# First attention of a hybrid block on one core: a chunk's scores in nine full steps, the diagonal blocks in two steps of their own, the later half of the queries first

## The chip, the core and the metric

The kernel runs on one core of a Trainium2 chip. The number that counts is the device time of one execution in microseconds (us). The five engines of a core that appear below are PE (TensorE, the matrix unit; PEld is its weight load), DVE (VectorE), ACT (ScalarE), POOL (GpSimd) and SP (SyncE, which here only issues DMAs). Each engine works through its own list of instructions in order. A matrix product writes into PSUM, eight banks of 512 fp32 columns on 128 partitions; DVE and ACT read it from there.

## What is computed

A block with four parts, each added to its input: attention A, an expert feed-forward part, attention B, and the same feed-forward part again. Only attention A is touched. It has 1024 tokens, 32 heads of 16 channels, rotary embedding and a causal mask:

```python
xq = rotary_pos_emb((x @ wq.T).reshape(B, T, n_heads, hd))
xk = rotary_pos_emb((x @ wk.T).reshape(B, T, n_heads, hd))
xv = (x @ wv.T).reshape(B, T, n_heads, hd)
scores = jnp.einsum('bqhd,bkhd->bhqk', xq, xk) * hd ** (-0.5)
scores = jnp.where(causal[None, None], scores, NEG_INF)
probs = jax.nn.softmax(scores, axis=-1)
out = jnp.einsum('bhqk,bkhd->bqhd', probs, xv).reshape(B, T, C) @ wo.T
```

## The kernel before

**Chunks.** The 32 heads are worked in eight chunks of four (`NCA` is 8, `HC` is 4). In `qT` and `kT` a chunk fills the 128 partitions with four strips of 32: 16 channels of a head, one row for the maximum, and zeros. A score product of one head therefore uses 32 rows of the matrix unit, and four heads in different strips run beside each other.

**Scores twice.** Softmax needs each query's maximum. The kernel makes every score twice. The *row* scores (`row_scores`, L310) have queries on partitions; DVE takes the maxima from them (`maxima`, L327 for a block without the mask, L330 for one with it). `with_maxima` (L345 to L350) turns the negated maxima of one half of the queries into rows (a transpose on PE, `tp_m`; a copy on ACT; four DMAs from SP) and writes them into the spare row of `qT`, where `kT` has ones. The *column* scores (`col_scores`, L362) have keys on partitions and get the maximum subtracted by that row. `exponentials` adds the causal mask with a bf16 product against the identity (L380) and lets ACT take the exponential into `p` (L382). `product` (L396) multiplies `p` with the values and a column of ones into `oT`, one PSUM bank (`ps_o`, one buffer) for the 512 queries of a half. When a half is done ACT copies it (L407), and `normalize` transposes it on PE (`tp_o`, L99), divides by the sums on DVE and POOL.

**Steps.** Queries come in halves `qc` of 512, keys and queries in blocks of 128. The lists `by_rows` and `by_cols` say what a step makes: a pair `(i, kc)` is row block `i` against the key half `kc`, a pair `(qc, b)` is key block `b` against query half `qc`, as wide as the mask leaves it (512, 384, 256 or 128). There are ten steps; two of them, n = 2 and n = 9, are 256 wide on both sides, the others 512. The order is the earlier half of the queries first (n = 0 to 2), then the later half (n = 3 to 9). The mask goes to the first 128 columns of each block on the diagonal: one such block in n = 0, 2, 7 and 9, two in n = 1 and 8.

**Half-steps.** While chunk c makes its column scores, chunk c+1 makes its row scores in the same step. `step` does so in two half-steps: column scores of heads 2 and 3 with row scores of heads 0 and 1, then the other way round. On PE a half-step is: the four score products beside each other, the mask products of two heads (if the step is on the diagonal), what is due (`tp_o`, `tp_m`), and half of the product of the step before the last. The score tiles come from a pool of seven banks, so that the four tiles of a half-step wait for banks of the two half-steps before it, which ACT or DVE has to have read.

**Ends.** The row scores of chunk 0 have no partner; they stand between the projections (three steps with the last query and key projections, seven with value projections `pj_v`). The last chunk makes column scores of all four heads at once, with no half-steps. `with_maxima` for the earlier half is done in step 5 of the rows, for the later half in step 1 of the next chunk; the column scores need them in step 0 and step 3.

Of the kernel before, what the change touches and what calls it, by code (L numbers as in the profile page):

```python
# [9 lines left out]
F32 = mybir.dt.float32  # L10
# [6 lines left out]
P = 128  # L17
# [47 lines left out]
class Block:  # L65
# [174 lines left out]
    def attend_a(self, ctx_pool, pt, work, ps_s, ps_o, qT, kT, v_p, project_qk, project_v, midway, tail):  # L240
        nc, tc = self.nc, self.tc
        HC = P // PADA
        with ExitStack() as ctx:
# [22 lines left out]

            by_rows = [[(3, 0)], [(2, 0), (0, 0)], [(1, 0)], [(4, 0)], [(5, 0)], [(6, 0)], [(7, 0)]]
            by_rows += [[(7, 1)], [(6, 1), (4, 1)], [(5, 1)]]  # L270
            by_cols = [[(0, 0)], [(0, 1), (0, 3)], [(0, 2)], [(1, 0)], [(1, 1)], [(1, 2)], [(1, 3)]]
            by_cols += [[(1, 4)], [(1, 5), (1, 7)], [(1, 6)]]
            NP = len(by_rows)
            negs, parts, outs = {}, {}, {}

            def neg(c, half):
# [15 lines left out]
                    yield *x, at, at + width(*x)  # L292
                    at += width(*x)

            def row_pieces(n):
                return list(placed(by_rows[n], lambda i, kc: min(QC, (i + 1) * P - kc * QC)))

            def col_pieces(n):
                return list(placed(by_cols[n], lambda qc, b: min(QC, (qc + 1) * QC - b * P)))

            def on_diagonal(qc, b):
                return b * P >= qc * QC

            def row_scores(c, n, heads, made):

                for j in heads:
                    made[j] = ps_s.tile([P, QC], F32, tag="s", name=f"s{c}_{n}_{j}")
                for i, kc, at, end in row_pieces(n):
                    for j in heads:
                        nc.tensor.matmul(  # L310
                            made[j][:, at:end],
                            lhsT=qT[rows_of(j), c, i * P : (i + 1) * P],
                            rhs=kT[rows_of(j), c, kc * QC : kc * QC + end - at],
                            start=True,
                            stop=True,
                        )
                        yield

            def maxima(c, n, heads, made):

                for j in heads:
                    for i, kc, at, end in row_pieces(n):
                        s, w = made[j][:, at:end], end - at
                        if i >= NT // 2 and kc == 0:
                            if (c, i) not in parts:
                                parts[c, i] = qk.tile([P, HC], F32, tag="part", name=f"part{c}_{i}", bufs=8)
                            nc.vector.tensor_reduce(parts[c, i][:, j : j + 1], s, AX.X, ALU.max, negate=True)  # L327
                            continue
                        junk = work.tile([P, QC], F32, tag="w", name=f"junk{c}_{i}_{j}")
                        nc.vector.tensor_tensor_reduce(  # L330
                            out=junk[:, :w],
                            in0=s,
                            in1=mask[:, QC - w :],
                            scale=-1.0,
                            scalar=parts[c, i][:, j : j + 1] if kc else -NEG,
                            op0=ALU.add,
                            op1=ALU.min,
                            accum_out=neg(c, i // 4)[:, j, i % 4 : i % 4 + 1],
                        )
# [14 lines left out]

            def col_scores(c, n, heads, made):

                pieces = col_pieces(n)
                for j in heads:
                    made[j] = ps_s.tile([P, QC], F32, tag="s", name=f"sT{c}_{n}_{j}")
                for x, (qc, b, at, end) in enumerate(pieces):  # L360
                    for j in heads:
                        nc.tensor.matmul(  # L362
                            made[j][:, at:end],
                            lhsT=kT[rows_of(j), c, b * P : (b + 1) * P],
                            rhs=qT[rows_of(j), c, (qc + 1) * QC - (end - at) : (qc + 1) * QC],
                            start=x == 0,
                            stop=x == len(pieces) - 1 and not on_diagonal(qc, b),
                        )
                        yield

            def exponentials(n, heads, made, p):
                pieces = col_pieces(n)
                end = pieces[-1][-1]

                if on_diagonal(*pieces[0][:2]):
                    step = pieces[-1][2] // P or 1
                    mask = maskT.unsqueeze(1).to_broadcast([P, len(pieces), P])
                    for j in heads:
                        to = made[j].rearrange("p (a k) -> p a k", k=P)[:, : (len(pieces) - 1) * step + 1 : step, :]
                        nc.tensor.matmul(to, lhsT=identb, rhs=mask, start=False, stop=True)  # L380
                for j in heads:
                    nc.scalar.activation(p[:, j, :end], made[j][:, :end], AF.Exp)  # L382

            def product(c, n, p):

                first, last = n in (0, 3), n in (2, NP - 1)
                pieces = col_pieces(n)
                qc, middle = pieces[0][0], pieces[-1][-1] // 2
                if first:
                    outs[c, qc] = ps_o.tile([P, QC], F32, tag="o", name=f"oT{c}_{qc}")  # L390
                o = outs[c, qc]
                for lo, hi in ((0, middle), (middle, 2 * middle)):
                    for _, b, at, end in pieces:
                        x0, x1 = max(lo, at), min(hi, end)
                        for j in range(HC if x0 < x1 else 0):
                            nc.tensor.matmul(  # L396
                                o[rows_of(j), QC - end + x0 : QC - end + x1],
                                lhsT=v_cols(b, c * HC + j),
                                rhs=p[:, j, x0:x1],
                                start=first and x0 == 0,  # L400
                                stop=last and x1 == 2 * middle,
                            )
                    yield
                if not last:
                    return
                oT = work.tile([P, QC], F32, tag="w", name=f"oTs{c}_{qc}")
                nc.scalar.copy(oT, o)  # L407
                later.append(lambda: normalize(c, qc, oT))

            def normalize(c, qc, oT):  # L410
                if not o_sb:
# [25 lines left out]
            later = []  # L437
            pending = []

            def step(rc, cc, n):  # L440


                p, made, madeT = None, {}, {}
                due = list(later)
                later.clear()
                if cc is not None:
                    p = pt.tile([P, HC, QC], F32, tag="p", name=f"p{cc}_{n}")
                    pending.append((cc, n, p))
# [2 lines left out]
                for half in range(2 if both else 1):  # L451
                    rows, cols = (2 * half, 2 * half + 1), (2 - 2 * half, 3 - 2 * half)
                    if not both:
                        rows = cols = range(HC)
                    gens = []
                    if cc is not None:
                        gens.append(col_scores(cc, n, cols, madeT))
                    if rc is not None:
                        gens.append(row_scores(rc, n, rows, made))
                    drain(gens)  # L460
                    if rc is not None:
                        maxima(rc, n, rows, made)
                    if cc is not None:
                        exponentials(n, cols, madeT, p)
                    while due:
                        due.pop(0)()
                    next(turns, None)
                drain([turns])
                if rc is not None and n == 4:
                    later.append(lambda: with_maxima(rc, 0))  # L470
                if cc is not None and n == 0:
                    later.append(lambda: with_maxima(cc, 1))


            for i in range(1, NT):
# [4 lines left out]
                next(project_v)  # L480
                step(0, None, n)
            for _ in project_v:
                pass
            for c in range(NCA):
                if c == NCA // 2:
                    midway()
                for n in range(NP):
                    step(c + 1 if c + 1 < NCA else None, c, n)
            for item in pending:
                drain([product(*item)])  # L490
            tail(o_sb, ps_s, work, later)
        return o_sb
# [493 lines left out]
def hybrid_block_kernel(  # L986
# [38 lines left out]
    def tail(o, ps, work, later):  # L1025
        oTs = [gather(o, i, work, ps, "w", "s") for i in range(2)]
        out_projection(0, oTs[0], ps, "s")
        while later:
            later.pop(0)()
        out_projection(1, oTs[1], ps, "s")  # L1030

    weights = [w_baseT, w_rhT, lora_B, b_base]
# [105 lines left out]
```

## Time and profile before

| | us |
|---|---|
| median of 3 runs (lowest, highest) | 1655.16 (1654.3, 1655.9) |
| the profiled execution | 1654.29 |
| its span, first to last instruction | 1652.2 |
| PE, DVE, ACT, POOL busy in the span | 1632.8, 1100.7, 555.2, 351.6 |
| chunk 0's first column scores | 119.12 |
| chunks 0 to 7 begin at | 119.12, 154.10, 190.71, 227.32, 263.94, 300.55, 337.16, 373.76 |
| the transposes that follow attention A (`tp_ao`) begin at | 401.31 |

The granted clock of TensorE is 1.000 for the whole span. A chunk's begin is the first column score product of its step 0 in the timeline. In the timeline a row begins with its start and its length in us; a row with x2 or more is several instructions run together. Each fp32 product of scores stands there as two passes. The length of a PE row holds its way through the array, so that the distance of two starts, not the length, tells what a product costs. Lines of code are those printed above.

### The profile page before, as it was taken

Reading aid. Unit: us, or ns where it says so; the run is one execution under the profiler, and the core shown is the slowest. Engines: PE = TensorE matmul, PEld = TensorE weight load, DVE = VectorE, ACT = ScalarE, POOL = GpSimd, SP = SyncE. Lnnn points to the kernel's source line nnn. Section 1 sums busy time; section 2 is a strip of 40 time slices with the busy share of each in tenths; the row PEclk is TensorE's granted clock in tenths of the full one; section 3 lists DMA queues with packets and bytes.
Section 4 is the critical chain, followed back from the end, with each engine's and each line's share of the span. In section 5 each row is a group of like instructions: output and inputs, shape, how many; then the busy total and the mean of one; then the engine's idle time right before and its main releaser. Section 6 shows DMA issues by size and latency. Waiting matters only on the chain.

```text
span 1652.2 us, 31905 instructions
## 1 busy us (share of the span) xinstructions
PE 1632.8 (99%) x12920; PEld 937.4 (57%) x12920; DVE 1100.7 (67%) x2832; ACT 555.2 (34%) x1230; POOL 351.6 (21%) x524
## 2 busy tenths in 40 slices
PE   9999999999999999999999999999999999999998
PEld 5544444444654657556655765655665576556654
DVE  4557777771553886776677677677667767777762
ACT  2325565555212333233233223223323322332230
POOL 3000000001311332223213222222322222222140
PEclk9999999999999999999999999999999999999999
DMA  5000000001003200200200120020020012000001
GB/s 198 1 1 2 3 2 2 2 2 40 1 27 88 65 1 27 65 27 26 65 27 7 51 60 2 27 65 26 27 65 26 16 45 64 1 27 27 2 1 51
DMA packets 60866, 52.03 MB, mean 31 GB/s; under 512 B 5744, under 2 KB 47472, under 8 KB 60720
## 3 DMA queue, kind: packets, MB, share of 16 engines
q1 hardware_dynamic: 59408, 46.06, 9.7%
q0 software_dynamic: 784, 2.90, 0.5%
q8 instruction: 101, 1.65, 0.4%
q10 hardware_dynamic: 528, 1.05, 0.2%
q14 instruction: 45, 0.37, 0.1%
HBM read 30.98 MB, written 2.10 MB: 20 GB/s over the span
## 4 chain that ended last, share of the span: by engine, by line
PE 95%; DVE 3%; ACT 1%; POOL 1%; issue 0%; ACTq 0%; DVEq 0%; POOLq 0%
PE s L798 15%; PE pq L752 13%; PE o L842 13%; PE wo L649 12%; PE sT L362 8%; PE kv L707 7%; PE oT L396 5%; PE pm_f L606 3%; PE or L842 3%; PE s L310 2%; PE pj_v L185 2%; PE pj_q L185 2%; PE pj_k L185 2%; PE sT L380 1%; PE pm_ao L1022 1%; PE st L778 1%
## 5 line engine op out<-in xcount | busy, mean ns | idle before, releaser
L807 ACT ACTIVATE p<-p,nm 128x1024 f32<-128x1024 f32 (+7 forms) x256 | 198.2, 774 | 405.3 <-DVE nm L805 363.6
L810 POOL TENSOR_SCALAR p<-p,rs 128x1024 f32<-128x1024 f32 (+7 forms) x256 | 190.9, 747 | 644.8 <-DVE rs L809 620.9
L798 PE MATMUL s<-kT,qT 128*128 128x512 f32 (+3 forms) x768 | 296.0, 493 | 1.9 <-DVE p L800 1.8
L825 DVE STREAM_TRANSPOSE pT<-p 128x640 f32<-128x640 f32 (+4 forms) x256 | 169.0, 670 | 128.6 <-PE o L842 84.5
L752 PE MATMUL pq<-xnTb,wq 128*128 128x512 f32 x512 | 243.0, 597 | 0.0
L649 PE MATMUL wo<-wo,oT 128*128 128x512 f32 x512 | 240.7, 593 | 1.8 <-DVE nm L805 1.8
L800 DVE SCALAR_TENSOR_TENSOR p<-s,rq,rel 128x512 f32<-128x512 f32 (+3 forms) x384 | 223.9, 601 | 24.6 <-PE s L798 23.4
L798 PEld LDWEIGHTS s<-kT,qT 128*128 128x128 f32 x768 | 140.8, 190 | 164.8 <-issue 117.7
L842 PEld LDWEIGHTS o<-pT,va 32*128 32x128 f32 x5248 | 210.7, 185 | 25.5 <-issue 17.9
L842 PE MATMUL o<-pT,va 32*128 32x256 f32 (+5 forms) x5248 | 220.0, 321 | 0.0
L382 ACT ACTIVATE p<-sT 128x512 f32<-128x512 f32 (+1 forms) x320 | 159.2, 554 | 107.1 <-PE sT L380 67.6
L804 DVE TENSOR_REDUCE nm<-p 128x1 f32<-128x1024 f32 (+7 forms) x256 | 188.7, 738 | 2.9
L310 PE MATMUL s<-kT,qT 32*128 32x512 f32 (+3 forms) x768 | 169.6, 524 | 0.0
L362 PE MATMUL sT<-qT,kT 32*128 32x512 f32 (+3 forms) x768 | 160.5, 524 | 0.0
L649 PEld LDWEIGHTS wo<-wo,oT 128*128 128x128 f32 x512 | 94.6, 190 | 89.0 <-issue 76.3
L752 PEld LDWEIGHTS pq<-xnTb,wq 128*128 128x128 f32 x512 | 92.4, 190 | 88.8 <-issue 79.7
L707 PE MATMUL kv<-wkv,xnTb 128*128 128x256 f32 x512 | 116.5, 380 | 0.8 <-DVE qT L762 0.5
L707 PEld LDWEIGHTS kv<-wkv,xnTb 128*128 128x128 f32 x512 | 96.3, 190 | 20.0 <-issue 4.0
L327 DVE TENSOR_REDUCE part<-s 128x1 f32<-128x512 f32 x128 | 82.0, 685 | 36.9 <-PE s L310 31.0
L362 PEld LDWEIGHTS sT<-qT,kT 32*128 32x128 f32 x768 | 61.5, 183 | 56.3 <-issue 37.8
L396 PE MATMUL oT<-p,v_p 128*32 128x256 f32 (+1 forms) x1408 | 93.0, 350 | 0.0
L421 POOL TENSOR_TENSOR o<-os,rsa 128x64 f32<-128x64 f32 x64 | 16.7, 293 | 338.5 <-DVE rsa L419 323.4
(154 smaller groups left out, 1623.2 us busy)
## 6 DMA issues: line engine op xcount, KB each, us to landing
va<-v SPq DMA_DIRECT2D x256, 64.0 KB
wq<-in_b_WqT_dram SPq DMA_DIRECT2D x8, 1024.0 KB
wo<-in_b_WoT_dram SPq DMA_DIRECT2D x8, 1024.0 KB
x<-in_x_dram SPq DMA_DIRECT2D x8, 256.0 KB
wkv<-in_b_WkT_dram SPq DMA_DIRECT2D x8, 256.0 KB
wkv<-in_b_WvT_dram SPq DMA_DIRECT2D x8, 256.0 KB
out_dram<-x SPq DMA_DIRECT2D x8, 256.0 KB
wq<-in_a_wqT_dram ACTq DMA_DIRECT2D x1, 1024.0 KB
```

The source lines that it names most:

```text
L310: nc.tensor.matmul(made[j][:, at:end], lhsT=qT[rows_of(j), c, i * P : (i + 1) * P], rhs=kT[rows_of(j), c, kc * QC : kc * QC + end - at], s ...
L362: nc.tensor.matmul(made[j][:, at:end], lhsT=kT[rows_of(j), c, b * P : (b + 1) * P], rhs=qT[rows_of(j), c, (qc + 1) * QC - (end - at) : (qc ...
L396: nc.tensor.matmul(o[rows_of(j), QC - end + x0 : QC - end + x1], lhsT=v_cols(b, c * HC + j), rhs=p[:, j, x0:x1], start=first and x0 == 0, ...
L649: nc.tensor.matmul(ps, lhsT=oTs[g, h][:, t * P : (t + 1) * P], rhs=wo[:, h, :], start=(h == heads[0]), stop=(h == heads[-1]))
L707: nc.tensor.matmul(ps.rearrange("p a b -> p (a b)"), lhsT=xnT[:, kc, i * P : (i + 1) * P], rhs=wkv[:, kc].rearrange("p a b -> p (a b)"), s ...
L752: nc.tensor.matmul(ps, lhsT=wq[:, kc, hh * DB : (hh + 1) * DB], rhs=xnT[:, kc, cols], start=(kc == 0), stop=(kc == KC - 1))
L798: nc.tensor.matmul(s, lhsT=qT[:, i * P : (i + 1) * P], rhs=kT[:, lo:hi], start=True, stop=True)
L800: nc.vector.scalar_tensor_tensor(p[:, lo:hi], s, rq[:, i : i + 1], rel[:, at + lo : at + hi], ALU.mult, ALU.add)
L804: nc.vector.tensor_reduce(nm, p[:, :w], AX.X, ALU.max, negate=True)
L807: nc.scalar.activation(p[:, :w], p[:, :w], AF.Exp, bias=nm, scale=slope, accum_out=ss)
L810: nc.gpsimd.tensor_scalar(p[:, :w], p[:, :w], rs, 1.0, ALU.mult, ALU.mult)
L842: nc.tensor.matmul(cols(o[:, a], j), lhsT=vs[g][rows, j * NB + b, :], rhs=moving(j, rows, slice(b * B, (b + 1) * B)), start=(j == js[0] an ...
```

## The change

`by_rows` and `by_cols` become functions of the chunk. There are nine steps where rows and columns go together. The four diagonal blocks of a query half (128 x 128 each) make one step of their own, `diagonal(qc)`; what stands beside them, to the right of the diagonal, makes `beside(qc, ...)`: blocks 0 and 2 (384 + 128) in one step, block 1 (256) in another. Every chunk but the last takes `down_cols`: the later half of the queries first, and the two 256-wide remainders, `beside(1, 1)` and `beside(0, 1)`, in one step. The last chunk takes `up_cols`: ten steps, the earlier half first. Rows of chunks 0 and 7 follow `up_rows`, the others `down_rows`; in both, (1, 0) and (5, 1) share a step. The mask is added once a diagonal step, over 512 columns for a head. `product` finds out itself where a half begins and ends; in the merged step its first half ends `qc` = 1 and its second half opens `qc` = 0. `with_maxima` is queued after the last step that a half's rows need, and is done in the first half-step after that; the queue `later` is now looked through in every half-step.

```diff
-            by_rows = [[(3, 0)], [(2, 0), (0, 0)], [(1, 0)], [(4, 0)], [(5, 0)], [(6, 0)], [(7, 0)]]
-            by_rows += [[(7, 1)], [(6, 1), (4, 1)], [(5, 1)]]
-            by_cols = [[(0, 0)], [(0, 1), (0, 3)], [(0, 2)], [(1, 0)], [(1, 1)], [(1, 2)], [(1, 3)]]
-            by_cols += [[(1, 4)], [(1, 5), (1, 7)], [(1, 6)]]
+            up_rows = [[(3, 0)], [(2, 0), (0, 0)], [(4, 0)], [(5, 0)], [(1, 0), (5, 1)], [(6, 0)], [(7, 0)], [(7, 1)]]
+            up_rows += [[(6, 1), (4, 1)]]
+            down_rows = [[(4, 0)], [(5, 0)], [(6, 0)], [(7, 0)], [(7, 1)], [(6, 1), (4, 1)], [(1, 0), (5, 1)], [(3, 0)]]
+            down_rows += [[(2, 0), (0, 0)]]
+            def diagonal(qc):
+                return [(qc, 4 * qc + a, a * P, (a + 1) * P) for a in range(4)]
+            def beside(qc, *blocks):
+                return [(qc, 4 * qc + a, (a + 1) * P, QC) for a in blocks]
+            full = [[(1, b, 0, QC)] for b in range(4)]
+            up_cols = [diagonal(0), beside(0, 0, 2), beside(0, 1), *full, diagonal(1), beside(1, 0, 2), beside(1, 1)]
+            down_cols = [*full, diagonal(1), beside(1, 0, 2), beside(1, 1) + beside(0, 1), diagonal(0), beside(0, 0, 2)]
+            def by_rows(c):
+                return up_rows if c in (0, NCA - 1) else down_rows
+            def by_cols(c):
+                return down_cols if c < NCA - 1 else up_cols
...
-                if on_diagonal(*pieces[0][:2]):
-                    step = pieces[-1][2] // P or 1
+                if pieces[0][:4] in diagonal(pieces[0][0]):
                     mask = maskT.unsqueeze(1).to_broadcast([P, len(pieces), P])
                     for j in heads:
-                        to = made[j].rearrange("p (a k) -> p a k", k=P)[:, : (len(pieces) - 1) * step + 1 : step, :]
+                        to = made[j].rearrange("p (a k) -> p a k", k=P)
                         nc.tensor.matmul(to, lhsT=identb, rhs=mask, start=False, stop=True)
...
                 for lo, hi in ((0, middle), (middle, 2 * middle)):
+                    for qc, b, x0, _, at, end in pieces:
+                        p0, p1 = max(lo, at), min(hi, end)
+                        if p0 >= p1:
+                            continue
+                        first = (c, qc) not in outs
+                        if first:
+                            outs[c, qc] = ps_o.tile([P, QC], F32, tag="o", name=f"oT{c}_{qc}")
...
+                        if last:
+                            oT = work.tile([P, QC], F32, tag="w", name=f"oTs{c}_{qc}")
+                            nc.scalar.copy(oT, o)
+                            later.append([0, lambda qc=qc, oT=oT: normalize(c, qc, oT)])
                     yield
...
+            def due():
+                for x in list(later):
+                    x[0] -= 1
+                    if x[0] < 0:
+                        later.remove(x)
+                        x[1]()
...
-                if rc is not None and n == 4:
-                    later.append(lambda: with_maxima(rc, 0))
-                if cc is not None and n == 0:
-                    later.append(lambda: with_maxima(cc, 1))
+                if rc is not None:
+                    for half in range(2):
+                        if n == max(m for m, y in enumerate(by_rows(rc)) for x in y if x[0] // 4 == half):
+                            later.append([0, lambda half=half: with_maxima(rc, half)])
...
             for _ in project_v:
-                pass
+                due()
             for c in range(NCA):
                 if c == NCA // 2:
                     midway()
-                for n in range(NP):
+                for n in range(len(by_cols(c))):
                     step(c + 1 if c + 1 < NCA else None, c, n)
             for item in pending:
+                due()
                 drain([product(*item)])
```

## The prediction

> **What bounds the kernel now.** I first read the windows, one for each chunk (bounds are the starts of the first column score product of a chunk; columns: length, then the busy time of PE, PEld, DVE, ACT, POOL).
>
> ```profile
> core 0: us, PE busy (x) PEld busy (x) DVE busy (x) ACT busy (x) POOL busy (x), PEclk, DMA share, GB/s
> ...
> 154.10:190.71 36.61, 36.33 (x406) 15.76 (x402) 25.89 (x83) 21.78 (x47) 2.09 (x8) 1.00 0.01 2
> 190.71:227.32 36.61, 36.34 (x406) 15.77 (x402) 25.88 (x83) 21.77 (x47) 2.09 (x8) 1.00 0.01 3
> ```
>
> Chunks 1 to 6 take 36.61 us each, to 0.02. PE is busy 99% of it, DVE 71%, ACT 59%, at full clock, and the page's chain of waits is 95% PE. So a chunk costs what PE's list costs, plus small waits that the busy time hides. To see both I read the timeline of one plain pair of half-steps (n = 3):
>
> ```profile
> 202.20 0.69 PE L362 MATMUL sT<-qT,kT 32*128 32x512 f32 x1
> ...
> 203.27 0.64 PE L396 MATMUL oT<-p,v_p 128*32 128x256 f32 x8
> ...
> 203.42 1.08 ACT L382 ACTIVATE p<-sT 128x512 f32<-128x512 f32 x2 [1.08 <-PE s L310]
> 203.84 0.69 PE L362 MATMUL sT<-qT,kT 32*128 32x512 f32 x1
> ...
> 204.07 0.69 PE L310 MATMUL s<-kT,qT 32*128 32x512 f32 x1
> ...
> 205.12 0.65 PE L396 MATMUL oT<-p,v_p 128*32 128x128 f32 x16
> ...
> 205.69 0.69 PE L362 MATMUL sT<-qT,kT 32*128 32x512 f32 x1
> ```
>
> Four score products of 512 columns side by side: 203.27 - 202.20 = **1.07** (call it S). Half of a value product: 203.84 - 203.27 = **0.57** (P), and 205.69 - 205.12 = 0.57 too where it is sixteen passes of 128 columns instead of eight of 256. The fourth score tile of the second half-step starts at 204.07 and not 203.84: its bank is read by the first exponential, 203.42 to 203.96. So S is 1.28 there, a wait of **0.2**. That pushes the next half-step back far enough not to wait itself; two plain half-steps take 205.69 - 202.20 = 3.49, and n = 6 takes 1.79 + 1.70 = 3.49 too. Then the masks (n = 7 and 8):
>
> ```profile
> 217.60 0.28 PE L380 MATMUL sT<-maskT,identb 128*128 128x128 bf16 x2
> 217.81 0.64 PE L396 MATMUL oT<-p,v_p 128*32 128x256 f32 x8
> ...
> 221.04 0.27 PE L362 MATMUL sT<-qT,kT 32*128 32x128 f32 x1
> ...
> 221.15 0.27 PE L362 MATMUL sT<-qT,kT 32*128 32x128 f32 x1
> ...
> 221.46 0.39 PE L380 MATMUL sT<-maskT,identb 128*128 128x256 bf16 x2
> 221.78 0.64 PE L396 MATMUL oT<-p,v_p 128*32 128x256 f32 x8
> ```
>
> The masks of two heads (M) cost 0.21 at 128 columns and 0.32 at 256, all of it on PE's path. A 128-wide score piece follows the one before on its strip after 0.11.
>
> From the same timeline: S of a 256-wide step 0.65, P of one 0.36, `tp_o` alone (T) 0.58, `tp_m` (X) 0.22. A chunk's account: S 16 x 1.07 + 4 x 0.65 = 19.72; P 16 x 0.57 + 4 x 0.36 = 10.56; M 8 x 0.21 + 4 x 0.32 = 2.96; T 1.16; X 0.44; together 34.84, so 1.77 of waits.
>
> **The change, part by part, for a chunk with both sides.**
>
> *Nine full steps for ten.* S becomes 18 x 1.07 = 19.26 (-0.46), P 18 x 0.57 = 10.26 (-0.30). The value products on 128-wide pieces cost no more, by the 0.57 above.
>
> *Masks.* Twelve half-steps with a mask become four, each with 512 columns a head. The trace has no such mask. The rows give 0.11 for 128 more columns on both heads, so 0.32 + 2 x 0.11 = 0.54. Below, it is no shorter than the 256-wide 0.32; above, no longer than four 128-wide pairs, 4 x 0.21 = 0.84. I take 0.54, on the line of both rows: M = 4 x 0.54 = 2.16 (-0.80). The bounds move a chunk by -0.9 to +1.2.
>
> *Diagonal steps.* A head has four pieces of 128 where it had one of 512, eight passes of 0.11, 0.88 in all, on a strip of its own, beside row products of 512 that need 1.07 anyhow. They are hidden, S stays 1.07: no gain is possible under the row products. If a 128-wide piece could not load its weights under the piece before, every pass would cost two times 0.11 and S about 1.07 + 8 x 0.11 = 1.9. The 0.11 between two such pieces in the fence above, each with weights of its own, says they can.
>
> *Waits.* DVE's heaviest half-step, (6, 1) with (4, 1), takes 1.70 in its timeline (221.47 to 223.17); (1, 0) with (5, 1) is put together from 256-wide rows, 2 x (0.35 + 0.41) = 1.52. Both are under the 1.74 of a plain half-step, so DVE doesn't become late although they now stand next to each other without masks between. The built program's list of waits shows that the last score tile of most half-steps still waits for the first exponential of the half-step before, so I keep 0.2 in every second plain half-step: seven of nine steps, 1.4. In diagonal half-steps the exponential starts later, but PE too: 0.54 of mask and 0.57 of product stand before the next scores, against about 0.5 + 0.54 until the first exponential is done: no wait. After X, 0.2 for DVE's second maximum. With 0.1 after T that is 1.7, as before.
>
> *T and X* are as many as before. X for the later half moves from the next chunk's n = 1 to n = 7, one half-step after the maxima it needs. These end 1.22 + 1.52 = 2.74 after their half-step's begin; PE gets to X, a plain half-step, S and M later, after 1.64 + 1.07 + 0.54 = 3.25: no wait. In the queue it then stands in front of one P and the second diagonal half-step; they would be late with it. Before, X at 232.44 was followed by the ACT copy at 233.56 and SP's first of four DMAs, spaced 0.67, and all had landed 4.7 after X. Now 0.57 + 2.19 + 3.5 + 0.6 = 6.9 us lie between X and the chunk's first column scores, so SP's four DMAs, each behind the other in SP's queue, stay hidden with 2 us to spare. The earlier half has six steps.
>
> *The merged step.* Its second P opens a new `oT` in the one bank. ACT has to have copied the old one: its exponentials end 2.30 after that step's begin in PE's next round (n = 8), the copy takes 0.59, T stands at 1.64 + 1.07 + 0.2 = 2.91. It is ready just then; if not, ACT's 0.1 to 0.3 is paid once a chunk.
>
> *Sum for a chunk:* 19.26 + 10.26 + 2.16 + 1.16 + 0.44 + 1.7 = 35.0, that is **-1.6**. Chunks 1 to 6: -9.6. Chunk 0 has no value products in its first two steps, before and after, and one X less: -1.8.
>
> *The ends.* Chunk 0 now needs the later half's maxima at once. X comes after the seventh value projection; the copy, the DMAs and their landing take 0.9 + 0.25 + 3.3 = 4.45, the X and the last projection, 0.2 + 3.6, cover 3.8: +0.65, once (0 to 1.5). The rows before it lose one half-empty step: -0.1. In the last chunk M is paid in two lumps of 4 x 0.28, in which ACT, at 2.07 of exponentials a step, has nothing to do, and X comes a step earlier, which takes away most of the wait at 382.3 to 383.6 for its DMAs; I put it at 0 (-1.5 to +1).
>
> Together -9.6 - 1.8 + 0.65 - 0.1 = **-10.8**. The profiled execution took 1654.29 us (span 1652.2): 1643.5. Taken from the median of the runs, 0.87 higher: **1644.4**. Everything behind attention A starts earlier by the same time; it is 99% PE and waits for nothing that has another clock, since its weights are loaded in buffers that attention A frees.
>
> **The rivals.**
>
> 1. *Weights don't hide under short pieces* (slower). A diagonal half-step then costs 0.85 more, 4 x 7 + 2 of them: +25.5, 1669.9. From 0.36 more per half-step on, the change loses. Against it stands the 0.11 between passes, on all four strips at once; for it, that the trace shows only one such piece after another on a strip, not four. The Trainium skill, TensorE: Matmul & The Clock Gate, "The mechanism", states this rule: a weight load overlaps with running products only when they are on other strips. By that rule the gap would be 0.21; the trace's 0.11 doesn't agree.
> 2. *The gain goes into PSUM waits.* If the 0.2 is paid in every plain half-step and not in every second, 7 more a chunk: 1.4 x 7 = 9.8, 1654: no change. If in half of them, 1649. For it: masks gave ACT time in twelve half-steps and now do in four. Against it: the pair always comes to 3.49 in the trace.
> 3. *The maxima come late.* The order is turned round and the column scores of the later half are wanted right at a chunk's begin. If the DMAs land 1 us after that instead of 2 before it, 7 us are lost: 1651. Against it: the 4.7 above, the same in every chunk.
>
> **How the numbers follow.** Forecast 0.72, with its own range 1640 to 1649 (the mask's bounds weighted to its line, the ends' bounds). Rival 1: 0.08. Rival 2: 0.12, half of it no change. Rival 3: 0.05. The remaining 0.03 is a slowdown I don't see. The range 1639 to 1653 leaves out rival 1, a part of rival 2 and what is unseen. A measurement of this kernel can tell about 0.2%, 3.3 us. Faster by more: 0.72 + 0.06 + 0.04 = 0.82. Within: 0.07. Slower: 0.11.
>
> **What would show it.** Chunks 1 to 5 begin 35.0 apart (34.4 to 35.6). The mask rows are 8 instructions a chunk, 0.27 to 0.28 from one to the next. The value product after a diagonal step's masks begins 1.6 to 1.7 after the first column score; 2.4 there means rival 1. Plain pairs at 3.6 or more mean rival 2. A gap of PE ahead of a chunk's first column score, ended by a DMA, means rival 3. The forecast is wrong if chunks are not shorter than 36.

## The result and the profile after

| us | before | changed |
|---|---|---|
| median of 4 runs (lowest, highest) | 1655.15 (1654.3, 1655.9) | 1641.41 (1639.48, 1641.65) |
| the profiled execution, its span | 1654.29, 1652.2 | 1641.65, 1639.6 |
| attention A: first column score to `tp_ao` | 119.12 to 401.31: 282.19 | 119.95 to 387.08: 267.13 |
| of it chunk 0, chunks 1 to 6, last chunk | 34.98, 219.66, 27.55 | 32.15, 208.76, 26.22 |
| from `tp_ao` to the last matmul | 1246.20 | 1247.89 |

The ratio of the times is 0.9915, 95% interval 0.9897 to 0.9932: 13.7 us less by the medians. The forecast was 1644.4.

The windows of the changed kernel by chunk, columns as before (bounds are again the first column score products): chunk 0, chunks 1 and 2, and the last one.

```profile
core 0: us, PE busy (x) PEld busy (x) DVE busy (x) ACT busy (x) POOL busy (x), PEclk, DMA share, GB/s
119.95:152.10 32.15, 32.15 (x390) 18.16 (x390) 24.73 (x79) 20.68 (x40) 0.00 (x0) 1.00 0.01 2
152.10:186.78 34.68, 34.68 (x454) 17.73 (x451) 25.69 (x85) 21.30 (x43) 2.09 (x8) 1.00 0.01 2
186.78:221.46 34.68, 34.68 (x454) 17.74 (x450) 25.68 (x85) 21.29 (x43) 2.09 (x8) 1.00 0.01 3
360.86:387.08 26.22, 24.37 (x429) 13.87 (x426) 1.17 (x7) 20.37 (x46) 3.13 (x12) 1.00 0.01 2
```

A chunk takes 34.68 where it took 36.61; PE is busy in all of it and has more instructions (454 for 406: the 128-wide pieces). DVE and ACT do what they did (25.7 and 21.3 for 25.9 and 21.8). Chunks 3 and 5 take 34.69 and 34.68, chunks 4 and 6 take 34.96 and 35.07. In chunk 4 one exponential starts 0.28 later in its half-step than in chunk 2, and the scores behind it take 1.56 for 1.29; why it is late stays open. Chunk 6 makes the rows of the last chunk, by `up_rows`, so that X stands in another step, and the scores behind it take 1.71.

The timeline of the changed kernel in two plain half-steps, the first with X, then one more begin:

```profile
186.78 0.69 PE L378 MATMUL sT<-qT,kT 32*128 32x512 f32 x1
...
187.85 0.28 PE L360 MATMUL tp_m<-ident,neg 128*16 128x128 f32 x1
188.00 1.09 ACT L397 ACTIVATE p<-sT 128x512 f32<-128x512 f32 x2 [1.11 <-PE s L325]
...
188.06 0.65 PE L417 MATMUL oT<-p,v_p 128*32 128x128 f32 x16
...
188.63 0.69 PE L378 MATMUL sT<-qT,kT 32*128 32x512 f32 x1
...
190.35 0.69 PE L378 MATMUL sT<-qT,kT 32*128 32x512 f32 x1
```

S is 187.85 - 186.78 = 1.07 and P 188.63 - 188.06 = 0.57, as before. The pair takes 190.35 - 186.78 = 3.57 with X's 0.21 in it; without X, plain pairs take 3.43 to 3.51. So X costs about 0.1 of its 0.21 there (0.06 to 0.14, by the pair it is held against). The rest fits time in which the next half-step would have waited for a bank. The diagonal half-step in the same kernel's timeline:

```profile
203.47 0.37 PE L378 MATMUL sT<-qT,kT 32*128 32x128 f32 x1
203.48 0.69 PE L325 MATMUL s<-kT,qT 32*128 32x512 f32 x1
...
203.68 0.51 PE L378 MATMUL sT<-qT,kT 32*128 32x128 f32 x6
...
204.03 0.60 PE L378 MATMUL sT<-qT,kT 32*128 32x128 f32 x7
...
204.57 0.60 PE L395 MATMUL sT<-maskT,identb 128*128 128x512 bf16 x2
...
205.00 1.08 ACT L397 ACTIVATE p<-sT 128x512 f32<-128x512 f32 x2 [1.06 <-PE sT L395]
...
205.10 0.64 PE L417 MATMUL oT<-p,v_p 128*32 128x256 f32 x8
...
205.68 0.58 PE L378 MATMUL sT<-qT,kT 32*128 32x384 f32 x1
```

The 128-wide pieces (x1, x6, x7, and more in lines left out) follow each other inside the time of the row products: S is 204.57 - 203.47 = 1.10. The mask (M) then takes 205.10 - 204.57 = 0.53.

Summed over every half-step of a chunk's timeline (work is a count times 1.07 or 0.65, the wait is what S takes beyond it):

| us per chunk | S work | waits in S | P | M | T waiting for ACT's copy | T + X | sum |
|---|---|---|---|---|---|---|---|
| before | 19.72 | 1.60 | 10.54 | 2.92 | 0.34 | 1.49 | 36.61 |
| changed | 19.26 | 1.52 | 10.28 | 2.05 | 0 | 1.58 | 34.69 |

### The profile page after: what moved, and what is told of

Read it like the earlier page. It is cut to its first block, busy times and chain, and to the rows that moved or that the text cites. A ratio compares the mean times of both kernels' runs of the same rounds, so it can differ in the third digit from the quotient of the medians.

```text
span 1639.6 us, 32629 instructions
## 1 busy us (share of the span) xinstructions
PE 1621.2 (99%) x13320; PEld 955.1 (58%) x13320; DVE 1099.2 (67%) x2832; ACT 551.5 (34%) x1202; POOL 350.8 (21%) x524
## 4 chain that ended last, share of the span: by engine, by line
PE 73%; DVE 3%; POOL 1%; ACT 1%; issue 0%; ACTq 0%; DVEq 0%
PE s L825 15%; PE pq L779 14%; PE o L869 13%; PE wo L676 13%; PE kv L734 7%; PE pm_f L633 3%; PE or L869 3%; PE pm_ao L1049 1%; PE st L805 1%; PE pm_f L634 1%; PE tp_k L99 0%; DVE p L827 0%; PE pr_f L568 0%; PE oT L417 0%; POOL x L559 0%; DVE pT L852 0%
## 5 line engine op out<-in xcount | busy, mean ns | idle before, releaser
L397 ACT ACTIVATE p<-sT 128x512 f32<-128x512 f32 (+1 forms) x292 | 155.7, 592 | 97.7 <-PE s L325 46.2
L325 PE MATMUL s<-kT,qT 32*128 32x512 f32 (+3 forms) x768 | 164.1, 520 | 0.0
L378 PE MATMUL sT<-qT,kT 32*128 32x128 f32 (+3 forms) x1152 | 155.4, 401 | 0.2 <-DMA qT<-negT 0.2
L378 PEld LDWEIGHTS sT<-qT,kT 32*128 32x128 f32 x1152 | 80.9, 184 | 50.8 <-issue 24.6
L417 PE MATMUL oT<-p,v_p 128*32 128x128 f32 (+1 forms) x1552 | 89.8, 332 | 0.0
```

The lines of the kernel that those rows point to most:

```text
L325: nc.tensor.matmul(made[j][:, at:end], lhsT=qT[rows_of(j), c, i * P : (i + 1) * P], rhs=kT[rows_of(j), c, kc * QC : kc * QC + end - at], s ...
L378: nc.tensor.matmul(made[j][:, at:end], lhsT=kT[rows_of(j), c, b * P : (b + 1) * P], rhs=qT[rows_of(j), c, qc * QC + x0 : qc * QC + x1], st ...
```

## The experiments

Every experiment starts from the changed kernel, whose chunk is 34.69 and whose attention A is 267.13 by its profile. Chunks and attention A are read from one profile each; a chunk's time is that of chunks 1 to 3, which agree to 0.02. Total times of single runs are given beside them; these differ by some 1.7 us by whether the execution has the half-clock stretch of the last section, so that attention A is what is compared.

### Is the mask paid by the instruction or by the half-step?

```diff
-                    mask = maskT.unsqueeze(1).to_broadcast([P, len(pieces), P])
-                    for j in heads:
-                        to = made[j].rearrange("p (a k) -> p a k", k=P)
-                        nc.tensor.matmul(to, lhsT=identb, rhs=mask, start=False, stop=True)
+                    for a in range(4):
+                        for j in heads:
+                            to = made[j][:, a * P : (a + 1) * P]
+                            nc.tensor.matmul(to, lhsT=identb, rhs=maskT, start=False, stop=a == 3)
```

> The changed kernel with one edit: in a diagonal step the mask of a head is added in four products of 128 columns instead of one of 512. Nothing else moves. In the changed kernel chunks 1 to 5 begin 34.69 us apart and the masks of a half-step (M) take 0.54. Theory A: a masked half-step pays once for turning the array from strips to whole and back (about 0.10), and then for columns alone (0.056 for 128 columns of a head): M = 0.10 + 8 x 0.056 = 0.55, chunks 34.7 (34.6 to 34.9). Theory B: each mask product has a price of its own, as the pairs of 0.21 before the change read: M = 4 x 0.21 = 0.84, four half-steps, chunks 35.9.

Chunk 34.73, attention A 267.52, total 1639.94. The timeline of this kernel's diagonal half-step, mask and then value product:

```profile
202.05 0.62 PE L395 MATMUL sT<-maskT,identb 128*128 128x128 bf16 x8
202.60 0.64 PE L417 MATMUL oT<-p,v_p 128*32 128x256 f32 x8
```

Eight products of 128 columns take 202.60 - 202.05 = 0.55 where two of 512 take 0.53. The number of instructions hardly matters: 0.02 for six more. With the old rows (0.21 for two heads of 128, 0.32 for two of 256) this gives one price: about 0.10 for each half-step that has a mask, and about 0.055 for each 128 columns. The upper bound of the prediction, four times 0.21, counted the 0.10 four times.

### The parts of the change, undone one by one

*The merged step undone* (ten steps, diagonal steps kept; `up_rows` and `down_rows` with (1, 0) and (5, 1) apart):

```diff
-            down_cols = [*full, diagonal(1), beside(1, 0, 2), beside(1, 1) + beside(0, 1), diagonal(0), beside(0, 0, 2)]
+            down_cols = [*full, diagonal(1), beside(1, 0, 2), beside(1, 1), beside(0, 1), diagonal(0), beside(0, 0, 2)]
```

> The changed kernel with the merge undone: (1, 0) and (5, 1) are steps of their own again among the rows, and beside(1, 1) and beside(0, 1) among the columns, so that a chunk has ten steps; diagonal steps and order stay. Theory A, the account by terms: scores +0.46 (4 x 0.65 - 2 x 1.07), value products +0.30 (4 x 0.36 - 2 x 0.57), waits as they are: chunks 1 to 5 begin 34.69 + 0.76 = 35.45 apart (35.2 to 35.7). Rival: the merge works through waits (fewer tiles in all): 36 or more. Other rival: the short steps give ACT and DVE time, which takes waits away again: 34.7 to 35.1.

Its windows, one chunk:

```profile
core 0: us, PE busy (x) PEld busy (x) DVE busy (x) ACT busy (x) POOL busy (x), PEclk, DMA share, GB/s
193.70:229.11 35.41, 35.41 (x470) 17.81 (x467) 25.82 (x83) 21.77 (x47) 2.09 (x9) 1.00 0.01 3
```

35.41 - 34.69 = 0.72. The account's S work (0.46) and P (0.25) make it up; M is 0.10 more and the waits are 0.09 less. Attention A grew by 275.08 - 267.13 = 7.95 from its first column score on: chunks 1 to 5 are 3.4 of it, chunk 0 is 2.7, chunk 6 is 1.8. The total is 1653.71, 12.3 above the changed kernel's median: chunk 0 also begins later, at 123.44, after a wait that the timeline names:

```profile
123.44 1.19 PE L378 MATMUL sT<-qT,kT 32*128 32x512 f32 x1 [3.77 <-DMA qT<-negT]
```

With a ten-step row list the transpose X of chunk 0's last maxima stands behind the last value projection, so that nothing covers its copy and its DMAs. That is the wait which the prediction priced at 0.65 for the changed kernel; there it was 0.24. The wait costs more than its own length: from 122.19 to 129.03 the granted clock is 0.50 (the product in the row lasts 1.19 where it lasts 0.69 at full clock), and the time from chunk 0's first column score to its first value product is 8.35 for 6.19 in the changed kernel. That is 2.2 of the 2.7 by which chunk 0 is longer.

*The diagonal steps undone* (nine steps and the merge kept, masks on the first 128 columns of each diagonal block again; the last chunk as it is):

```diff
-            down_cols = [*full, diagonal(1), beside(1, 0, 2), beside(1, 1) + beside(0, 1), diagonal(0), beside(0, 0, 2)]
+            def wide(qc, *blocks):
+                return [(qc, 4 * qc + a, a * P, QC) for a in blocks]
+
+            down_cols = [*full, wide(1, 0), wide(1, 1, 3), wide(1, 2) + wide(0, 2), wide(0, 0), wide(0, 1, 3)]
```

> The changed kernel with the diagonal steps undone in all chunks but the last: each key block keeps its 128 diagonal columns, so that nine steps stay (the two 256-wide ones share a step), later half first, but five of them carry masks on one or two blocks. Theory A: M = 2 x (0.21 + 0.32 + 0.32 + 0.21 + 0.32) = 2.76 for 2.16: chunks 34.69 + 0.60 = 35.3 (35.1 to 35.5). Rival: more masked half-steps give ACT time and take away the wait of 0.2 for the first exponential in three more pairs: 34.7.

Its windows, one chunk, and the timeline of half-steps with masks:

```profile
core 0: us, PE busy (x) PEld busy (x) DVE busy (x) ACT busy (x) POOL busy (x), PEclk, DMA share, GB/s
186.28:221.05 34.77, 34.77 (x386) 14.87 (x382) 25.82 (x85) 21.30 (x44) 2.09 (x8) 1.00 0.01 2
```

```profile
201.86 0.28 PE L401 MATMUL sT<-maskT,identb 128*128 128x128 bf16 x2
202.08 0.64 PE L423 MATMUL oT<-p,v_p 128*32 128x256 f32 x8
202.65 0.69 PE L381 MATMUL sT<-qT,kT 32*128 32x512 f32 x1
...
203.72 0.28 PE L401 MATMUL sT<-maskT,identb 128*128 128x128 bf16 x2
...
204.51 0.58 PE L381 MATMUL sT<-qT,kT 32*128 32x384 f32 x1
...
205.72 0.39 PE L401 MATMUL sT<-maskT,identb 128*128 128x256 bf16 x2
```

34.77: only 0.08 more, where 0.6 more was expected from the price of the masks. M did grow, by 2.63 - 2.05 = 0.58. But the waits in S fell from 1.52 to 1.11, all of it in the last four steps: the longer S of each pair there is 205.72 - 204.51 = 1.21, then 1.22, 1.15 and 1.09, where the changed kernel has 1.27 to 1.29. This fits ACT reading a bank while PE spends 0.22 to 0.32 on a mask. The diagonal steps, in a kernel of nine steps, give 0.08 a chunk; attention A is 267.48 and the total 1639.65.

*The order undone* (earlier half first, nine steps; all rows `up_rows`):

```diff
-            down_cols = [*full, diagonal(1), beside(1, 0, 2), beside(1, 1) + beside(0, 1), diagonal(0), beside(0, 0, 2)]
+            down_cols = [diagonal(0), beside(0, 0, 2), beside(0, 1) + beside(1, 1), *full, diagonal(1), beside(1, 0, 2)]
...
-                return up_rows if c in (0, NCA - 1) else down_rows
+                return up_rows
```

> Nine steps and diagonal steps as in the changed kernel, but the earlier half of the queries first in every chunk (diagonal(0), beside(0, 0, 2), beside(0, 1) with beside(1, 1), the four full steps, diagonal(1), beside(1, 0, 2)), with up_rows for all rows. Theory A: the order has no price of its own. The later half's maxima are transposed in the next chunk's step 0, 1.6 after its begin, their DMAs land 4.7 after that, at 6.3; step 2, which needs them, begins at 4.5 + 3.5 = 8.0: no wait, chunks 34.7 (34.4 to 35.0). Rival: the order is what makes nine steps possible, since the maxima come late: PE waits 1 us or more ahead of step 2, chunks 35.7 or more.

Chunk 34.79, attention A 267.74, total 1639.51. The first column score, at 118.82, waits for no DMA. The order is worth little by itself in this form: 0.10 a chunk for it, and a wait of 0.24 once against it.

### How late may the maxima be?

For chunks 1 to 6, X of the later half two half-steps later:

```diff
-                            later.append([0, lambda half=half: with_maxima(rc, half)])
+                            later.append([2 * half * (0 < rc < NCA - 1), lambda half=half: with_maxima(rc, half)])
```

> The changed kernel with the later half's maxima of chunks 1 to 6 put into their row two half-steps later (the transpose X moves from the first half-step of n = 7 to that of n = 8; the copy and the four DMAs with it). Theory A: in the changed kernel 7.0 us lie between X and the next chunk's begin and 4.7 are needed, so 2.3 are to spare; two half-steps are 4.0, so that PE waits 1.7 ahead of a chunk's first column score: chunks 1 to 5 begin 34.69 + 1.7 = 36.4 apart (35.9 to 36.9), PE's wait ended by the DMA qT<-negT, and the run loses some 10 us of its gain. Rival: the DMAs are sooner there than 4.7: 34.7 to 35.2.

Its timeline around a chunk's begin:

```profile
223.08 2.57 SPq L365 DMA_DIRECT2D qT<-negT  x4
...
224.63 0.64 PE L417 MATMUL oT<-p,v_p 128*32 128x256 f32 x8
...
226.06 0.69 PE L378 MATMUL sT<-qT,kT 32*128 32x512 f32 x1 [0.80 <-DMA qT<-negT]
```

Chunk 36.48 (36.4 was expected), attention A 280.09: 13 us more, total 1652.76. The bracket at the last row says that PE stood 0.80 idle before the chunk's first column score, and that a DMA ended it. That is not the whole price: the scores of that half-step then take 1.82 for 1.07, because two of its four score products start only at 226.82 (the four DMAs come one behind the other). X two half-steps later, 4.0 us, costs 1.8 a chunk: so about 2 us were spare, as the prediction had it for rival 3. Six times 1.8 is 10.8 of the 13 us. The rest lies around the begin of chunk 4, where PE waits 1.56 and then has a granted clock of 0.50 for 3.4 us; chunks 3 and 4 take 37.27 and 38.02. Rival 3 did not happen, but its price was real: this delay gives back most of what the change brings.

### What are the 1.5 us of waits?

Exponentials at half width. The second half of each exponential is left out and the first is used twice:

```diff
-                    nc.scalar.activation(p[:, j, :end], made[j][:, :end], AF.Exp)
+                    nc.scalar.activation(p[:, j, : end // 2], made[j][:, : end // 2], AF.Exp)
...
-                                rhs=p[:, j, p0:p1],
+                                rhs=p[:, j, p0 - lo : p1 - lo],
```

> The changed kernel with exponentials of half the width: ACT works on the first half of each score tile, the second half of the exponentials is left out and the first half stands in for it in the value products. PE and DVE do the same work as before. Theory A: the 0.2 that every second plain half-step waits is the first exponential of the half-step before, which frees the bank of the fourth score tile; at 0.33 for 0.54 it is done in time, and some 1.3 of the 1.5 us of waits in a chunk's score products go: chunks 33.4 (33.1 to 33.7). Rival: DVE's maxima free that bank last, or the wait is PE's own change between tilings: 34.7.

Timeline of this kernel, two plain half-steps:

```profile
187.69 0.69 PE L378 MATMUL sT<-qT,kT 32*128 32x512 f32 x1
...
188.76 0.64 PE L417 MATMUL oT<-p,v_p 128*32 128x256 f32 x8
188.84 0.66 ACT L397 ACTIVATE p<-sT 128x256 f32<-128x256 f32 x2 [1.06 <-PE s L325]
...
189.33 0.69 PE L378 MATMUL sT<-qT,kT 32*128 32x512 f32 x1
...
190.40 0.64 PE L417 MATMUL oT<-p,v_p 128*32 128x128 f32 x16
...
190.97 0.69 PE L378 MATMUL sT<-qT,kT 32*128 32x512 f32 x1
```

Half-steps of 189.33 - 187.69 = 1.64 and 190.97 - 189.33 = 1.64, as the account of PE's work alone has it (1.07 + 0.57). Chunk 33.59, 1.10 less, attention A 257.83, total 1630.09. So some 1.1 of the 1.52 are banks that wait for the exponentials; 0.2 of what is left stands in one half-step of the second diagonal step, where DVE's maximum is late.

The mask left out instead, with the exponentials' input scaled by 2 to the -10:

```diff
-                            stop=x == len(pieces) - 1 and not masked,
+                            stop=x == len(pieces) - 1,
...
-                if pieces[0][:4] in diagonal(pieces[0][0]):
...
-                        nc.tensor.matmul(to, lhsT=identb, rhs=mask, start=False, stop=True)
...
-                    nc.scalar.activation(p[:, j, :end], made[j][:, :end], AF.Exp)
+                    nc.scalar.activation(p[:, j, :end], made[j][:, :end], AF.Exp, scale=2.0**-10)
```

> The changed kernel without the mask products in the column scores; the mask is left out there, and the exponent is scaled down so that it stays finite. Theory A: M is PE's own time and goes with its whole 2.05: chunks 34.69 - 2.05 + 0.1 = 32.75 (32.5 to 33.1). Rival, from the spread masks, where 0.55 more of M took 0.41 of waits away: mask time is mostly time in which ACT catches up, three quarters of it come back as waits: chunks 34.2.

Chunk 33.22, attention A 254.89, total 1628.75: between the two expectations. M of 2.05 is gone, and the chunk is 1.47 shorter; the waits in S went from 1.52 to 2.09. So masks in diagonal steps are mostly paid (1.47 of 2.05). Spread masks, in the experiment above, were mostly covered: 0.58 more of mask time cost 0.08.

### Filling the waits

What can fill a wait costs less than its length: X beside a plain half-step costs about 0.1. So T of the later half was put one half-step later, beside X. In the last chunk, where the profile shows PE waiting for `oTs`, the copy went from ACT to DVE, which is nearly idle there (1.17 us busy in the window of the last chunk).

```diff
-                            nc.scalar.copy(oT, o)
-                            later.append([0, lambda qc=qc, oT=oT: normalize(c, qc, oT)])
+                            last_chunk = c + (qc == 0) >= NCA - 1
+                            (nc.vector.tensor_copy if last_chunk else nc.scalar.copy)(oT, o)
+                            delay = 1 if qc and c < NCA - 1 else 0
+                            later.append([delay, lambda qc=qc, oT=oT: normalize(c, qc, oT)])
```

> The changed kernel with two edits meant to use waits. The output transposes of the later half (tp_o) are done one half-step later, in the first half-step of the next chunk together with X, and in the last chunk the finished half is copied by DVE, which is idle there, and not behind ACT's exponentials. Theory A: T in the second half-step of n = 8 (2.44) comes after that half-step's wait and hides nothing; beside X it hides what a plain pair waits: the two steps n = 8 and n = 0 take 3.50 + 3.98 for 4.09 + 3.57, chunks 34.5; the last chunk loses the waits of 0.67 and 1.04 ahead of its two tp_o: 24.6 for 26.2. In all 2.5 to 3 us less than the changed kernel. Rival: the last chunk is bound by ACT's exponentials, and the wait comes back in its next steps: nothing there, 1 us in all.

The waits of the changed kernel from 360 to 388 (waiting operation and line, what it waited for; us in total, times, longest):

```profile
PE tp_o L99 <- ACT oTs L426: 1.9, 2, 1.0
```

and of this one from 358 to 384:

```profile
PE tp_o L99 <- DVE oTs L427: 0.3, 1, 0.3
```

Chunk 34.58 (0.11 less, 0.18 was expected), last chunk 24.97 for 26.22 although it has a T more in it, attention A 264.41: 2.72 less. In single runs this is 1638.12. As the totals of single runs move by 2 us for a reason of their own (last section), the two kernels were run again side by side, four executions each beside seven of the kernel before.

> The changed kernel as it is, timed in five rounds. By the profiled executions attention A takes 267.1 us for 282.2, and some executions lose 1.7 us near the end, where the granted clock is 0.5 for 3.4 us. Theory: a ratio of 0.9905 to 0.9925, that is 12.5 to 15.5 us less than before, with single runs some 2 us apart. If the profiled gain were of one execution only: nearer to 0.995.

> The version with the later output transposes and DVE's copies in the last chunk, timed in five rounds beside the changed kernel. Its attention A took 264.4 us for 267.1 in the profile. Theory: 2.7 us less than the changed kernel, ratio to before 0.989 to 0.991. Rival: what single runs lose to the clock near the end covers it, and the two intervals overlap.

| us | median | lowest, highest | ratio to before | 95% interval |
|---|---|---|---|---|
| before, beside them | 1656.36 | 1654.57, 1656.6 | | |
| changed, again | 1640.49 | 1639.6, 1641.57 | 0.9906 | 0.9889 to 0.9922 |
| with the waits filled | 1637.82 | 1637.0, 1638.7 | 0.9891 | 0.9877 to 0.9906 |

The medians are 2.7 apart, which is what the profiles show in attention A (267.13 and 264.44 in these runs), and every run of the one lies below every run of the other. The intervals of the ratios overlap, so that the totals alone would not settle it; the profiles of attention A do.

## Why the prediction was right, by its own steps

The direction, the mechanism and the bounds held. The mechanism is PE's list getting shorter in each chunk, with the full gain on the path. The forecast was 10.8 less; the medians show 13.7 less, and attention A alone 15.06. Chunks, chunk 0, the DMA wait and the last chunk all came out better than forecast. That the median still lies within the forecast's own range of 1640 to 1649 is luck in part: the profiled execution loses 1.7 us behind attention A, for a reason that is not of the change (last section), and the one execution of the four with a mean granted clock of 1.000 took 1639.48. The terms:

- *A chunk*: 1.6 less predicted (35.0), 1.92 measured (34.69). S work (-0.46) and P (-0.30, measured -0.26) are as counted. M was predicted at 0.54 a half-step and measured 0.53 to 0.54, 0.44 where X follows: -0.80 became -0.87. The mis-sized term is the **waits**, carried over "as before" (1.77 to 1.7 in the prediction, 1.94 to 1.52 in the account). T's wait of 0.34 for ACT's copy, in one half-step of n = 2, went away: T now stands elsewhere in the order and finds the copy done. The waits in S came out near as a sum, 1.60 before and 1.52 after, but not in the forecast pattern of 0.2 in every second plain half-step: after the change they are 0.06 to 0.08 in each of four half-steps of the first steps, and 0.15 to 0.22 in six others.
- *Chunks 1 to 6*: -9.6 predicted, -10.9 measured, which is the above six times, less 0.6 in chunks 4 and 6.
- *Chunk 0*: -1.8 predicted, -2.83 measured. The step carried P over from the full chunks, as -0.30. But of the steps whose products fall into chunk 0 there were seven full ones and one half-width one before, and there are seven full ones after: P 8.69 and 7.98, that is -0.71. And the waits in S, taken as equal, fell from 2.75 to 2.07; this lies ahead of the first value product, where they fell from 1.60 to 0.84.
- *The DMA wait at chunk 0*: +0.65 predicted; PE waited 0.24. The first column score stands 0.83 later in the profile, but the transposes at the very start already came 0.66 later in that execution.
- *The last chunk*: 0 predicted (-1.5 to +1), -1.33 measured. M is 1.84 for 2.36, and the wait of 1.2 for X's DMAs is gone, as the prediction had it; against this PE waits 0.5 longer ahead of its two T, for ACT's copies. The lumps of mask came to 0.87 and 0.97, where the prediction had 4 x 0.28.
- *Rival 1*, weights that don't hide: S of the diagonal half-step is 1.10, not 1.9. In the prediction's fence the two rows that are 0.11 apart are the two passes of one piece on a strip, each with its own load, and not two pieces; that whole pieces follow each other so is first seen here. The Trainium skill, TensorE: Matmul & The Clock Gate, "The mechanism", says that a weight load overlaps with running products only where the row strips differ; the four pieces on one strip, each with weights of its own, do not agree. The same section's sentence that a load may also go ahead into a background weight buffer fits them.
- *Rival 2*, the gain going into waits, did not happen either, but its reason is half right. Taking the masks out of the plain half-steps did bring waits back: the experiment with spread masks has 0.41 less of them. So the term "M -0.80" of the sum is not a gain by itself. Undone alone, the diagonal steps cost 0.08 a chunk, the merge 0.72, the order 0.10. With all undone, and the places of T and X with them, it is the kernel before, 1.92 away: single prices of parts that cover the same waits do not add up to the whole. The accounts show where the difference lies. From the kernel before to the one with spread masks, the waits (in S and for ACT's copy) fall from 1.94 to 1.11; with the diagonal steps they rise again to 1.52. The prediction has neither move; that the second gives back half of the first, and so keeps its sum near, is luck. What took away the first 0.83, T's 0.34 apart, was not tried part by part.
- *Everything behind attention A* "earlier by the same time": the tail is 1.7 longer, 1247.89 for 1246.20, for a reason that has nothing to do with the change (last section). In the profiles of six of the experiments it is 1246.16 to 1246.26, with the same code behind attention A; in the other five profiles with the change it is 1.4 to 2.3 longer than before, and each has a stretch at a lower granted clock in it.

Left open: why one exponential of chunk 4 is late, and which part of the change took most of the waits away. A mask that costs PE nothing, made by another engine behind the exponential, was not tried.

## What to carry to other kernels

Where one engine is busy all the time and still waits a little for a partner, an edit's price is its work minus the wait that it covers: masks of 0.22 to 0.32 in half-steps that would have waited 0.2 were nearly free (0.08 for 0.58), and four of 0.53 were mostly paid (1.47 of 2.05). Price a change by the account of the whole loop (work and waits, half-step by half-step), and test its parts one by one before crediting one of them. A step taken out whole (here a tenth of the score work that ran half empty) is worth its full time, and it also moves everything that was timed against its length: look at the one place where a transfer had only that step to hide behind.

## What was not expected of the hardware

**A stretch at half clock.** The changed kernel's windows near the end of the execution, in the router of the last feed-forward part:

```profile
core 0: us, PE busy (x) PEld busy (x) DVE busy (x) ACT busy (x) POOL busy (x), PEclk, DMA share, GB/s
1594.60:1598.07 3.47, 1.44 (x6) 0.78 (x6) 2.88 (x10) 0.97 (x2) 1.44 (x2) 1.00 0.00 0
1598.07:1601.48 3.41, 3.41 (x5) 1.35 (x4) 0.57 (x1) 0.00 (x0) 0.00 (x0) 0.50 0.00 0
1601.48:1605.00 3.52, 3.52 (x18) 2.18 (x17) 0.69 (x1) 0.86 (x2) 0.00 (x0) 1.00 0.19 74
```

After 3.47 us in which PE was busy for 1.44, the granted clock (the column PEclk) is 0.50 for 3.41 us and 1.00 again. At half clock 3.41 us of products do what takes 1.7 at full clock, and the tail is 1.7 longer. It is not of the change: of seven executions of the kernel before that ran beside the last experiments, five have a mean clock of 0.999 and take 1656.24 to 1656.6, two have 1.000 and take 1654.57 and 1654.67; of the changed kernel's four, two have 0.999 (1640.96 and 1641.57) and two 1.000 (1639.6 and 1640.01). Between executions at 1.000 the change is worth about 15 us, which is what attention A shows. The Trainium skill, TensorE: Matmul & The Clock Gate, "What's actually happening", gives the gate's window as 3413 ns, free-running, with half clock behind an idle one; the trace agrees with the length, though PE was not idle for the whole of the 3.47 us. Two experiments have such a stretch where PE waits for DMAs: 6.84 us in the kernel with ten steps and 3.41 in the one with late maxima. In the 3.41 us ahead of the three stretches PE was busy for 1.4 (here), 0.9 and 1.8. These waits so cost more than they last, 2.2 us more in the one and some 1.3 in the other; the waits of 0.80 at other chunk begins had no such stretch behind them. From what busy share on the clock falls is not shown.

**The price of a mask product** has a fixed part of about 0.10 for a half-step, where products of strips give way to products over the whole array and come back, however many mask products stand there. That it is this turn which costs it was not tried by itself. It fits that where T or X follows at once, and not a value product, about 0.09 of it is missing: a mask takes 0.44 for 0.53 in the changed kernel, and T takes 0.50 for 0.58 in the kernel before. **Short score pieces** cost nothing beside long ones: eight passes of 128 columns on a strip with four sets of weights took 1.10 beside row products of 1.07.
